# Matmuls without a reader in three waits, four buffers for layer 1's key chunks, and a square moved behind two copies, in a four-layer convolution sequence

## The chip, the cores and the metric

The kernel runs on one core of one Trainium2 chip, in float32 throughout. The metric is the device time of one execution in microseconds (us), given as the median of several runs. Nothing is shared with other cores.

## The reference

The input is `x`, four images (B = 4) of 192 channels on 64x64 pixels. Four layers follow each other, and each works on all four images:

```python
# layer 0: deformable 3x3 convolution gives q; k, v are 1x1; channel attention; then an MLP
xn  = layer_norm(xs);  q = deform_conv(xn, w_p, b_p, w_d)
out = softmax(qh @ l2norm(kh).T * temperature) @ l2norm(vh);  xs2 = xs + proj(out)
xs3 = xs2 + gelu(layer_norm(xs2) @ w_fc1 + b_fc1) @ w_fc2 + b_fc2
# layer 1: non-local block over all 4096 pixels, 96 channels
f1 = theta(x).T @ phi(x);  y = softmax(f1, -1) @ g(x);  x = W(y) + x
# layer 2: layer norm, qkv, attention in overlapping 8x8 windows (6 heads), gated MLP
y = conv1x1(ln_c(x), qkv);  win = unfold(y, 8, stride 6, pad 3)
out = fold(exp(q k^T + bias - max) v) / fold(sums);  x1 = x + hft(proj(out));  x = x1 + gated_mlp(ln_c(x1))
# layer 3: one masked depthwise 3x3 convolution whose weights depend on the image's mean
```

## The kernel before

The images are taken one after the other; `b` is the image. For each one the program makes layer 1's keys and values, runs layer 1, the windows of layer 2, and then the rest of layer 2 with layer 3. Beside that it works ahead on layer 0 of image b + 1: its gathers run inside layer 1 (`weave`), and its MLP (`mlp0`) inside the rest of layer 2 and layer 3 (`rest`). Image 0's own layer 0 has nothing beside it, and for the last image (b = 3) there is no next layer 0.

The order of instructions on each engine comes from a planner that works with costs and due times. Only the window loop is issued in the order in which it is written (`tc.manual_schedule()`). Tiles come from pools; a tile's buffer is free for the next tile of its tag when all readers and writers of the old one are done, and an instruction that writes it waits for that.

Four places matter here.

**The end of `mlp0`.** It goes over eight chunks of 512 pixels (`CN`). For each, `narrow(1)` (L821) and `narrow(0)` (L818) project the hidden layer back to 192 channels in PSUM tiles `o2` (shown as `o` in the profile), VectorE adds bias and residual (L825), and SyncE stores the chunk to the DRAM array `x_flat`, shown as `xd` (L844).

**`keys`** (L849). It reads the same array back in eight chunks `xk` of 384 KB (L855), from a pool `l1k` of two buffers, and makes the keys `ph` (two matmuls, L858, of 96 rows, 96 columns of the array and 512 moving columns) and the values `gx` (eight matmuls, L863, of 96 moving columns). For b = 1 and 2 it alternates with `offsets(b + 1)`, layer 0's first norm of the next image. For b = 0 and 3 it runs alone. For b = 0, 1 and 2 layer 1's gathers of layer 0 (L572, on POOL's queue) may begin at the same time, and the loads `xc` of layer 1's queries (L899) are on SyncE's queue.

**The end of `layer1`.** For each of 16 groups of queries the sums `y` (L976) are copied from PSUM by ScalarE (L982), then `finish` runs a reciprocal (L942), one matmul `pd`, a product, and two matmuls `wy` with an addition each (L950, L951).

**The start of `windows`** (L993). Window row 0 needs `norm(0)`, whose steps are the generator `layer_norm_steps`: mean by matmul `pm` (L360), difference on VectorE (L364), square on ScalarE (L367), variance by matmul `pv` (L339) and square root on ScalarE (L372), reciprocal on VectorE (L374), spreading by matmul `pb` (L348), product on VectorE (L382). `norm(wr, upto)` runs the generator up to the named step (MEAN, DIFFERENCE, SQUARE, VARIANCE, INVERSE). Then `project_rows` makes queries and keys (`qk`, L1064 and L1065, copied by ScalarE, L1068 and L1070). In the loop each row `wr` has three groups `g` of four windows and each group two pairs; `turned` makes the values `v` (L1139) and turned weights `t` (L1147), each in a PSUM buffer of tag "a" (two buffers, shared with `qk`), and ScalarE copies both out (`vs`, L1144, and `et`, L1149). At the start of row `wr` the norm of row `wr + 2` is run up to SQUARE.

Of the kernel before, what the change touches and what calls it, by code (L numbers as in the profile page):

```python
# [10 lines left out]
F32 = mybir.dt.float32  # L11
# [7 lines left out]
B, C, H, W = 4, 192, 64, 64  # L19
# [60 lines left out]
def conv_seq_kernel(ctx: ExitStack, tc: tile.TileContext, a, out: bass.AP):  # L80
# [437 lines left out]
    def gather(b, s, at, m2, kept=None):  # L518
# [166 lines left out]
            nc.scalar.copy(m2[rows, C + 2 * M + Q * q : C + 2 * M + Q * q + Q], pm[rows, M:C])  # L685
        yield

    def mlp0(b, m2, pool, sb, ps):


# [96 lines left out]
        for i in range(NCH):  # L787
            x = xs.pop(i)
            gl = pool.tile([128, 6, CN], F32, tag="gl", name=f"gl_{b}_{i}")

            def widen(ms):

                banks = [ps.tile([128, 2, HN], F32, tag="h", name=f"h_{b}_{i}_{ms[0]}_{q}") for q in range(2)]
                for j, m in enumerate(ms):
                    for q in range(2):
                        nc.tensor.matmul(
                            banks[q][:, j, :], lhsT=fc1[:, 0, bass.ts(m, 128)], rhs=hn[:, bass.ts(q, HN)], start=j == 0,
                            stop=False, skip_group_check=True,
                        )
                for j, m in enumerate(ms):  # L800
                    for q in range(2):
                        rows = slice(Q * q, Q * q + Q)
                        nc.tensor.matmul(
                            banks[q][:, j, :], lhsT=fc1[rows, 1, bass.ts(m, 128)], rhs=hn[rows, CN:], start=False, stop=True,
                            skip_group_check=True,
                        )
                for j, m in enumerate(ms):
                    for q in range(2):
                        nc.scalar.activation(
                            gl[:, m, bass.ts(q, HN)], banks[q][:, j, :], AF.Gelu, bias=fc1_bias[:, m : m + 1]  # L810
                        )

            def narrow(k):

                p = ps.tile([128, CN], F32, tag="h", name=f"o2_{b}_{i}_{k}")[:, 0 : HN if k else CN]
                for m in range(6):
                    if k == 0:
                        nc.tensor.matmul(p, lhsT=fc2[:, m, 0:M], rhs=gl[:, m, :], start=m == 0, stop=m == 5)  # L818
                        continue
                    for q in range(2):  # L820
                        nc.tensor.matmul(  # L821
                            p[Q * q : Q * q + Q], lhsT=fc2[:, m, M:C], rhs=gl[:, m, bass.ts(q, HN)], start=m == 0, stop=m == 5
                        )
                to = x[:, CN:] if k else x[:, 0:CN]
                nc.vector.scalar_tensor_tensor(to, p, VW["l0_bfc2"][:, k], to, ALU.add, ALU.add)  # L825


            if i + 1 < NCH:
                attend(i + 1)
            widen((0, 1))  # L830
            yield
            norm(i + 1, MEAN)
            widen((2, 3))
            norm(i + 1, SQUARE)
            yield
            widen((4, 5))
            norm(i + 1, VARIANCE)
            narrow(1)
            norm(i + 1, INVERSE)
            yield  # L840
            hn = norm(i + 1)
            narrow(0)
            for of, to in parts(x, HN, x_flat[b % 2], CN * i):
                nc.sync.dma_start(out=to, in_=of)  # L844
            if i + 2 < NCH:
                load(i + 2)
            yield
# [22 lines left out]
    def layer1(b, kv, beside):  # L870

        ph, gx = kv
        with ExitStack() as s:
# [83 lines left out]
            def next_scores(k):  # L957
                if k < NQ * NG:
                    i, g = divmod(k, NG)
                    if g == 0:  # L960
                        load(i)
                    score(i, g)
                    if g == NG - 1:
                        mbs[i] = negated_max(i)
# [3 lines left out]
            for k in range(NQ * NG):  # L968
                i, g = divmod(k, NG)
                if g == 0:  # L970
                    py = ps1.tile([P + 1, QN], F32, tag="y", name=f"y_{b}_{i}")
                ex = slot(i, g)
                nc.vector.tensor_tensor(ex, ex, mbs[i].unsqueeze(1).to_broadcast([128, G, QN]), ALU.add)  # L973
                nc.scalar.activation(ex, ex, AF.Exp)  # L974
                for t in range(G):
                    nc.tensor.matmul(  # L976
                        py, lhsT=gx[:, G * g + t, :], rhs=ex[:, t, :],
                        start=g == 0 and t == 0, stop=g == NG - 1 and t == G - 1,
                    )
                if g == NG - 1:  # L980
                    y = sb.tile([P + 1, QN], F32, tag="yn", name=f"yn_{b}_{i}")
                    nc.scalar.copy(y, py)  # L982
                    ends.append((k, i, y))
                next_scores(k + ahead)
                if ends and (k >= ends[0][0] + 2 or k == NQ * NG - 1):
                    finish(*ends.pop(0)[1:])
                if beside is not None:
                    beside(k + 1)
# [4 lines left out]
    def windows(b, oi, load_image):  # L993
# [3 lines left out]
        with ExitStack() as s:  # L997
# [225 lines left out]
            pos, ots, inv = {}, {}, {}  # L1223
            groups = -(-NWIN // WG)
            with tc.manual_schedule():
                norm(0)
                shared(0, 0)
                project_rows(0, 0)
                norm(1, SQUARE)
                project_rows(0, 1)  # L1230
                norm(1, VARIANCE)
                queries(0)
                inputs(0)
                norm(1)
                shared(1, 0)
                load(2)
                ex = exponentials(0, 0, scores(0, 0))
                due = None
                for wr in range(NWIN):
                    for g in range(groups):  # L1240
                        nxt = (wr, g + 1) if g + 1 < groups else (wr + 1, 0)
                        if wr + 2 < NWIN and g == 0:
                            norm(wr + 2, SQUARE)
                        if nxt[0] < NWIN:
                            sc = scores(*nxt)
                        if wr + 3 < NWIN and g == 1:
                            load(wr + 3)
                        if wr + 2 < NWIN and g == 2:
                            norm(wr + 2)
                        for pair in range(WG // 2):  # L1250
                            ops = turned(wr, g, pair, ex)
                            if due is not None:
                                outputs(*due)
                                if g == 0 and pair == 0:
                                    collect(wr - 1)
                            due = ops
                            if g == 0 and wr + 1 < NWIN:
                                project_rows(wr + 1, pair)
                            if wr > 0 and g == 1 and pair == 0:
                                inverses(wr - 1)  # L1260
                            if wr > 0 and g == 2:
                                finish(wr - 1, pair)
                        if wr + 2 < NWIN and g == 1:
                            norm(wr + 2, INVERSE)
                        if nxt[0] < NWIN:
                            ex = exponentials(*nxt, sc)
                        if g == 0 and wr + 1 < NWIN:
                            for i in (1, 2):
                                shared(wr + 1, i)
                            queries(wr + 1)  # L1270
                            inputs(wr + 1)
                        if g == 2 and wr + 2 < NWIN:
                            shared(wr + 2, 0)
                    if wr == 1:
                        load_image()
                outputs(*due)
                collect(NWIN - 1)
                inverses(NWIN - 1)
                for h in range(2):
                    finish(NWIN - 1, h)  # L1280
# [579 lines left out]
    for b in range(B):  # L1860
        with ExitStack() as s:
# [5 lines left out]
                m2 = stats.tile([M, C + 3 * M], F32, tag="m2", name=f"m2_{b + 1}")  # L1867
            with ExitStack() as s2:
                making = keys(
                    b, ph, gx, s2.enter_context(pool_of(name="l1k", bufs=2)),  # L1870
                    s2.enter_context(pool_of(name="l1kps", bufs=2, space=PSUM)),
                )
                if 0 < b < B - 1:
                    parts = offsets(b + 1, sb)
                    for _ in range(NCH):
                        next(parts)
                        next(making, None)
                    at = links(parts)
                for _ in making:
                    pass  # L1880
# [96 lines left out]
```

## Time and profile before

| what | value |
|---|---|
| time, median of 3 runs | 7006.99 us (6996.74 to 7022.0) |
| the profiled execution's own time | 6945.72 us |
| its span, first to last instruction | 6943.9 us |
| TensorE (PE) busy, weight loads (PEld) | 6255.0 us (90%), 4231.5 us |
| VectorE (DVE), ScalarE (ACT), GpSimd (POOL) | 4819.6, 3728.4, 2070.6 us |
| matmul records on PE | 45020 |
| mean granted TensorE clock | 0.928 |

One float32 matmul shows as two records in the profile: `keys` calls 64 matmuls at L858 over the four images, and the profile has 128 records of them. "PEclk" is the share of TensorE's full clock that was granted. A line of the timeline gives start, busy time, engine, source line, operation, tiles out<-in, form, and in brackets the idle time before it with what ended it. A line of the stretches gives the stretch, its length, busy time and count for each engine, the granted clock, the DMA engines' busy share and GB/s.

### The profile page before, as it was taken

The page shows a single profiled execution, that of the slowest core. Times are in us where ns is not written, and L with a number is a line of the kernel's source. Part 1 is how long each engine was busy: PE and PEld are TensorE (multiplying, and loading weights), DVE is VectorE, ACT ScalarE, POOL GpSimd, SP SyncE. Part 2 cuts the span into 40 slices and gives each one's busy share as a digit, 9 for nine tenths or more (in the row PEclk, how much of TensorE's full clock was granted, in tenths as well). Part 3 has the DMA queues.
Part 4 walks back from the last instruction along what each step waited for, and adds up shares of the span by engine and source line. Part 5 has one row for each costly group of instructions (what it writes and reads, how often), then busy time and mean ns, then how long its engine had stood idle before and what let it go on. Part 6 is the DMA issues. An engine that isn't in the chain of part 4 may idle for free.

```text
span 6943.9 us, 114885 instructions
## 1 busy us (share of the span) xinstructions
PE 6255.0 (90%) x45020; PEld 4231.5 (61%) x45020; DVE 4819.6 (69%) x7087; ACT 3728.4 (54%) x6214; POOL 2070.6 (30%) x2273
## 2 busy tenths in 40 slices
PE   7878999998987899999988889999998889999876
PEld 4545588885543468886644458887654457766532
DVE  3763199975677669984586849995577757755656
ACT  3763288864444368873544348884544325545331
POOL 2762077732200057751200017772210000012100
PEclk8889899998999899998989999999999979999998
DMA  7993267731010287761010067773010010010000
GB/s 234 302 350 115 74 196 231 232 118 35 24 29 14 72 258 222 231 196 35 10 42 14 28 215 221 226 230 96 13 30 21 19 48 12 12 36 12 4 7 20
DMA packets 362108, 743.43 MB, mean 107 GB/s; under 512 B 52647, under 2 KB 245335, under 8 KB 360798
## 3 DMA queue, kind: packets, MB, share of 16 engines
q0 software_dynamic: 95616, 469.38, 21.0%
q1 hardware_dynamic: 265950, 266.70, 12.9%
q8 instruction: 355, 5.82, 0.3%
q14 instruction: 187, 1.53, 0.1%
HBM read 628.06 MB, written 106.21 MB: 106 GB/s over the span
## 4 chain that ended last, share of the span: by engine, by line
PE 63%; DVE 19%; ACT 7%; DMA 6%; issue 4%; SPq 1%; POOL 0%; DVEq 0%; ACTq 0%; POOLq 0%
PE s L910 11%; PE y L976 10%; PE h L590 6%; DMA ring<-table,idx 3%; PE v L1139 2%; PE qk L1064 2%; DVE ha L1308 2%; PE qk L1065 2%; PE h L1508 2%; DVE ga L1308 2%; PE t L1147 1%; PE tp L858 1%; PE po L482 1%; DVE gate L1308 1%; DVE row L579 1%
## 5 line engine op out<-in xcount | busy, mean ns | idle before, releaser
L572 POOL DMA_INDIRECT ring<-table,idx x1188 | 1673.2, 1408 | 1019.5 <-DVE row L579 235.0
L910 PE MATMUL s<-ths,ph 96*128 96x256 f32 x4096 | 981.8, 385 | 9.0 <-ACT sc L912 4.3
L910 PEld LDWEIGHTS s<-ths,ph 96*128 96x128 f32 x4096 | 782.6, 193 | 148.6 <-ACT ths L904 16.9
L578 ACT ACTIVATE row<-ring,pos 128x384 f32<-128x384 f32 x1188 | 699.0, 610 | 252.6 <-DVE xo L583 159.3
L579 DVE SCALAR_TENSOR_TENSOR row<-ring,fr,row 128x384 f32<-128x384 f32 x1188 | 699.2, 613 | 115.9 <-ACT row L578 109.9
L976 PE MATMUL y<-sc,gx 128*97 128x256 f32 x3008 | 720.1, 379 | 0.0
L976 PEld LDWEIGHTS y<-sc,gx 128*97 128x97 f32 x3008 | 489.0, 164 | 125.7 <-issue 2.3
L582 ACT ACTIVATE xo<-row,pos 128x192 f32<-128x192 f32 x1188 | 503.8, 448 | 74.5 <-DVE row L579 42.4
L583 DVE SCALAR_TENSOR_TENSOR xo<-row,fr,xo 128x192 f32<-128x192 f32 x1188 | 463.9, 410 | 40.3 <-ACT xo L582 38.7
L590 PE MATMUL h<-ti,xo 128*128 128x192 f32 x2376 | 460.6, 329 | 5.8 <-DVE xo L583 5.8
L912 ACT COPY sc<-s 128x1024 f32<-128x1024 f32 x376 | 376.8, 1002 | 158.9 <-PE s L910 157.6
L973 DVE TENSOR_TENSOR sc<-sc,mbs 128x1024 f32<-128x1024 f32 x376 | 446.5, 1216 | 14.0 <-ACT mbs L936 13.7
L917 DVE TENSOR_TENSOR top<-top,sc 128x1024 f32<-128x1024 f32 x282 | 344.5, 1222 | 147.8 <-ACT sc L912 147.3
L590 PEld LDWEIGHTS h<-ti,xo 128*128 128x128 f32 x2376 | 404.7, 191 | 40.1 <-DVE xo L583 12.9
L974 ACT ACTIVATE sc<-sc 128x1024 f32<-128x1024 f32 x376 | 392.9, 1054 | 44.8 <-DVE sc L973 43.0
L1123 DVE TENSOR_REDUCE es<-ex 128x6 f32<-128x384 f32 x264 | 133.3, 546 | 404.2 <-ACT ex L1119 404.2
L1549 POOL COPY gate<-gate 128x192 f32<-128x192 f32 x12 | 4.2, 348 | 1106.1 <-ACT gate L1542 1106.1
L590 PE MATMUL h<-kept,xo 128*128 128x192 f32 x990 | 255.7, 391 | 80.2 <-DVE xo L583 73.4
L1308 DVE SCALAR_TENSOR_TENSOR ga<-gate,v,ga 128x1024 f32<-128x1024 f32 x234 | 299.7, 1281 | 7.2
L590 PEld LDWEIGHTS h<-kept,xo 128*128 128x128 f32 x990 | 180.4, 216 | 167.7 <-DVE xo L583 135.9
L976 PE MATMUL y<-se,gx 128*97 128x256 f32 x1088 | 260.4, 379 | 0.5 <-ACT yn L982 0.5
L1187 POOL TENSOR_TENSOR ot<-ot,ot 102x128 f32<-102x128 f32 x80 | 54.9, 699 | 624.0 <-ACT ot L1181 623.7
(384 smaller groups left out, 11615.0 us busy)
## 6 DMA issues: line engine op xcount, KB each, us to landing
ti<-table SPq DMA_DIRECT2D x396, 96.0 KB
table<-tt SPq DMA_DIRECT2D x24, 1056.0 KB
ring<-table,idx POOLq DMA_INDIRECT x1188, 5.1
xnd<-xn SPq DMA_DIRECT2D x4, 3270.0 KB
table<-kept SPq DMA_DIRECT2D x12, 1056.0 KB
table<-tt SPq DMA_DIRECT2D x44, 288.0 KB
xi<-in_x_dram SPq DMA_DIRECT2D x32, 384.0 KB
xk<-xd SPq DMA_DIRECT2D x32, 384.0 KB
```

The lines of the kernel that those rows point to most:

```text
L572: nc.gpsimd.indirect_dma_start(out=gt.rearrange("p r q c -> p (r q c)"), out_offset=None, in_=table[:, :], in_offset=bass.IndirectOffsetOn ...
L578: nc.scalar.activation(row, gt[:, :, 0, :], AF.Copy, scale=pos[:, t, 9 + tap : 10 + tap])
L579: nc.vector.scalar_tensor_tensor(row, gt[:, :, 1, :], fr[:, t, 9 + tap : 10 + tap], row, ALU.mult, ALU.add)
L582: nc.scalar.activation(xo[:, j, :], row[:, 0, :], AF.Copy, scale=pos[:, t, tap : tap + 1])
L583: nc.vector.scalar_tensor_tensor(xo[:, j, :], row[:, 1, :], fr[:, t, tap : tap + 1], xo[:, j, :], ALU.mult, ALU.add)
L590: nc.tensor.matmul(acc[m // 2][:, bass.ts(m % 2, C)], lhsT=xo.rearrange("p j c -> p (j c)")[:, bass.ts(m, 128)], rhs=tt, start=t == 0 and ...
L910: nc.tensor.matmul(p[:, t, :], lhsT=ph[:, bass.ts(G * g + t, 128)], rhs=ths[i], start=True, stop=True)
L912: nc.scalar.copy(to, p)
L973: nc.vector.tensor_tensor(ex, ex, mbs[i].unsqueeze(1).to_broadcast([128, G, QN]), ALU.add)
L974: nc.scalar.activation(ex, ex, AF.Exp)
L976: nc.tensor.matmul(py, lhsT=gx[:, G * g + t, :], rhs=ex[:, t, :], start=g == 0 and t == 0, stop=g == NG - 1 and t == G - 1,)
L1308: nc.vector.scalar_tensor_tensor(acc[:, b], src(tap, b), w[:, tap : tap + 1], acc[:, b], ALU.mult, ALU.add)
```

## The change

A helper `keep_warm(p, n)` issues `n` matmuls into a PSUM tile `p` that nothing reads: identity as weights, and as many columns of the constant `bias` as `p` is wide. It is called

- in `mlp0` after the last chunk's store: 12 matmuls of 384 columns into the tile of `narrow(0)`;
- in `layer1` after the last copy of `y`: 4 matmuls of 256 columns into that `y`;
- in `windows` during `norm(0)`: 2, 2 and 1 matmuls of 384 columns, into a tile of their own of tag "a", behind the mean, behind the variance, and behind the spreading.

Further, the pool `l1k` has four buffers in place of two for the first and the last image; and in window row 0 only the mean of `norm(2)` is run at the start, its difference and square follow behind `project_rows(1, 0)`.

```diff
+    def keep_warm(p, n):
+        m, width = p.shape
+        columns = bias.rearrange("p e h j -> p (e h j)")[:, 0:width]
+        for _ in range(n):
+            nc.tensor.matmul(p, lhsT=ident[:, 0:m], rhs=columns, start=True, stop=True)
...
                 nc.vector.scalar_tensor_tensor(to, p, VW["l0_bfc2"][:, k], to, ALU.add, ALU.add)
+                return p
...
-            narrow(0)
+            p = narrow(0)
             for of, to in parts(x, HN, x_flat[b % 2], CN * i):
                 nc.sync.dma_start(out=to, in_=of)
+            if i == NCH - 1:
+                keep_warm(p[:, 0:384], 12)
...
                     ends.append((k, i, y))
+                    if i == NQ - 1:
+                        keep_warm(py, 4)
...
             with tc.manual_schedule():
+                warm = ps2.tile([128, 512], F32, tag="a", name=f"warm_{b}")[:, 0:384]
+                norm(0, MEAN)
+                keep_warm(warm, 2)
+                norm(0, VARIANCE)
+                keep_warm(warm, 2)
                 norm(0)
+                keep_warm(warm, 1)
...
                         if wr + 2 < NWIN and g == 0:
-                            norm(wr + 2, SQUARE)
+                            norm(wr + 2, SQUARE if wr else MEAN)
...
                             if g == 0 and wr + 1 < NWIN:
                                 project_rows(wr + 1, pair)
+                            if wr == 0 and g == 0 and pair == 0:
+                                norm(2, SQUARE)
...
-                    b, ph, gx, s2.enter_context(pool_of(name="l1k", bufs=2)),
+                    b, ph, gx, s2.enter_context(pool_of(name="l1k", bufs=2 if 0 < b < B - 1 else 4)),
```

## The prediction

> **What bounds the kernel.** I read the page first: the slices of the span, then the chain that ended last.
>
> ```profile
> PEclk8889899998999899998989999999999979999998
> PE 63%; DVE 19%; ACT 7%; DMA 6%; issue 4%; SPq 1%; POOL 0%; DVEq 0%; ACTq 0%; POOLq 0%
> ```
>
> TensorE carries the chain, and its clock is below full in most slices. The mean of 0.928 stands for (1 - 0.928) x 2 x 6944 = 1000 us at half clock. So I asked the stretches where the half clock lies, for the keys of images 0 and 3 and for image 0's windows:
>
> ```profile
> 807.09:864.00 56.91, 56.21 (x164) 37.53 (x164) 4.46 (x8) 5.93 (x9) 9.46 (x10) 0.50 0.42 132
> 5621.22:5678.00 56.78, 56.22 (x165) 37.34 (x165) 4.46 (x8) 5.92 (x9) 0.00 (x0) 0.50 0.24 68
> 1556.86:1573.94 17.08, 11.86 (x42) 6.32 (x43) 3.84 (x8) 2.87 (x4) 5.01 (x8) 0.50 0.10 31
> 1573.94:1587.58 13.64, 9.80 (x157) 6.11 (x155) 7.77 (x11) 4.77 (x8) 4.25 (x14) 1.00 0.08 23
> 1587.58:1601.24 13.66, 12.87 (x60) 6.37 (x61) 2.38 (x3) 3.55 (x8) 1.78 (x5) 0.50 0.97 242
> 1601.24:1614.89 13.65, 11.05 (x294) 7.88 (x292) 8.98 (x13) 8.69 (x15) 3.54 (x12) 1.00 0.06 15
> 1614.89:1635.36 20.47, 20.14 (x146) 10.51 (x146) 5.09 (x7) 5.27 (x11) 2.23 (x7) 0.50 0.06 15
> 1635.36:1867.47 232.11, 216.06 (x4385) 145.47 (x4384) 142.79 (x204) 122.97 (x229) 57.89 (x162) 1.00 0.05 15
> ```
>
> PE is 99% busy through both key stages (56.2 of 56.9 and 56.8 us), all at 0.50: nothing but the clock bounds them. The windows lose it three times and then keep it for 232 us. The timelines show what a chunk costs cold (image 0) and warm (image 1):
>
> ```profile
> 801.69 0.75 DVE L825 SCALAR_TENSOR_TENSOR xa<-o,wide,xa 128x512 f32<-128x512 f32 x1 [4.83 <-PE o L818]
> 802.89 0.89 SPq L855 DMA_DIRECT2D xk<-xd  x2
> 807.09 3.73 PE L858 MATMUL tp<-xk,phiT 96*96 96x512 f32 x4 [5.44 <-DMA xk<-xd]
> 810.62 3.57 PE L863 MATMUL g<-gT,xk 96*128 96x96 f32 x16
> ...
> 2380.51 1.92 PE L863 MATMUL g<-gT,xk 96*128 96x96 f32 x16
> 2382.27 1.88 PE L858 MATMUL tp<-xk,phiT 96*96 96x512 f32 x4
> ```
>
> A cold chunk recurs every 6.78 us; a warm one takes half of the 3.42 us of `tp` and 54% of the 3.36 us of `g`, 3.5 us.
>
> [...] stretches at 0.50 and 1.00 only, their limits whole multiples of 3.41 us apart. [...] the drop at 1587.58 came after 1.7 us idle. I weighted every matmul's streaming time by rows x columns / 128 squared: the 100 windows that ended in a drop have at most 0.40 (median 0.21). Pure key chunks weigh about 0.56, enough to hold a full clock; they never raised it, while dense full windows elsewhere did. [...] the chunk issued at 814.22 moved nothing before 816 while the gathers moved 400 GB/s.
>
> **Part 1, `mlp0`.** 48 matmuls over four images. A 384-column matmul is two records; two warm `qk` records of 384 columns take 0.66 us (1684.26 to 1684.92), so 12 take 7.9 us. They wait for L825, which reads their tile. Queued behind them on PE is only the first key chunk, which waits for its DMA anyway:
> - b = 0: L825 ends 802.4, they end at 810.4; chunk landed 807.1: 3.3 us late.
> - b = 1: 2359.7, 2367.8; landed 2367.8: not late.
> - b = 2: 3996.8, 4004.9; landed 4004.9: not late.
> - b = 3: 5614.7, 5622.8; landed 5621.2: 1.5 us late.
>
> PE idles about 1.2 us ahead of them, too little for a drop, so the keys begin warm.
> - b = 0: eight chunks take 28.2 instead of 54.2 us: -26; two `th` -1; layer 1's first scores, cold until 870.8, -3.4; late start +3.3: -27.
> - b = 3: -26, `th` -0.9, scores cold until 5683.6 -2.8, +1.5: -28.
> - b = 1, 2: cold from 2367.8 to 2379.4 and 4004.9 to 4017.9, where `offsets` let it rise: half, -5.8 and -6.5.
>
> Sum -67. What follows is layer 1, bound by PE in steady state, so it shifts whole.
>
> **Part 2, buffers.** No DMA is added; the 32 loads move ahead on SyncE's queue. With two buffers a warm chunk (3.5 us) would wait for loads of about 4 us, and in image 0 for 816 and later. With four, three chunks follow the first at once, 1.6 MB by about 809 at the 250 GB/s seen there, ahead of the gathers. The `xc` loads behind them on SyncE's queue come later; the chunk that reuses the first buffer is issued near 814, lands near 823 and is needed near 825. Bounds: 0 if it is in time, +13 us if PE idles over 1 us in one window and the rest goes cold. I take +3.
>
> **Part 3, `layer1`.** Four 256-column matmuls at 0.45 us (34 `y` records took 7.58 us) are 1.8 us per image. They wait for the copy and lie beside the 1.75 us reciprocal; behind them only `pd`, which waits for that. Cost about 0, bounds 0 and +0.3.
>
> **Part 4, `norm(0)`.** Groups of 1.3, 1.3 and 0.66 us lie in PE's gaps of 1.7, 1.6 and 0.6 us (ahead of `pv`, `pb`, `qk`). With parts 3 and 4 the stretch from 1556.9 to 1573.9 runs warm: `pd`, one `wy`, `pm`, `pv`, `pb` and four `qk` halves save 0.5 + 0.5 + 1.1 + 0.3 + 0.7 + 2 = 5 us. In between lies 2.9 us with only `pd` and `wy`, which may still drop; then the dense matmuls raise the clock in one window. Bounds -5.3 and +1; I take -4.5, four times -18.
>
> **Part 5, the moved square.** The gap it removes:
>
> ```profile
> 1586.24 0.94 DVE L364 TENSOR_TENSOR d_l2n<-xr,pm_l2n 96x768 f32<-96x768 f32 x1
> 1587.27 0.84 ACT L367 ACTIVATE sq_l2n<-d_l2n 96x768 f32<-96x768 f32 x1 [2.00 <-DVE d_l2n L364]
> 1588.02 0.30 ACT L1144 COPY vs<-v 128x192 f32<-128x192 f32 x1
> 1588.37 1.59 PE L1064 MATMUL qk<-xs,qkvT 96*96 96x384 f32 x2 [2.49 <-ACT vs L1144]
> ```
>
> `qk` waits for a PSUM buffer, which waits for `vs`, queued on ScalarE behind the square, which waits for VectorE. Without that, `vs` ends at 1585.6 and `qk` starts at 1585.9, 2.5 us earlier. The square is next late: behind three VectorE steps of row 0's scores it ends near 1591.1, and the second pair's `vs` and `qk` wait, some 0.9 us. The scores at 1601.8 come at 1594.1 warm: -7.7. With a drop in one of five cases (some +8) I take -6, four times -24.
>
> **The third drop**, at 1614.89, has its own gap (1.70 us, PE waiting for VectorE's L382), which stays. In before it fell at the same place in all four images, but 4 windows after a rise, so the positions were not independent. Now they are; I give 45% that it is held. Warm, the stretch costs 11.2 (1675.1 to 1686.3) instead of 20.5 us: -9.3 x 0.45 x 4 = -17; bounds 0 and -37.
>
> **Sum.** -67 + 3 - 18 - 24 - 17 = -123 in the profiled execution. I take off 8 for waits of the added groups that no row shows: -115, to about 6830 (span 6829). The median of the runs shown lies 61 us above the profiled execution; I assume that this stays: 7007 - 115 = 6892.
>
> **Rivals.**
> - Partly held (chance 0.26): one of the pure key stages drops after a late chunk, which alone costs up to 20 us, and the windows find drops elsewhere. For it: the weight 0.56 allows only about 1 us idle in a window. Time about 6950.
> - The change doesn't do what it says (0.07): the planner places the added matmuls elsewhere, or the windows ahead are low enough for the drop to come all the same, with the extra matmuls mostly in idle time. Against it: L825 holds them at the right place. About 7000.
> - Slower (0.05): the drop comes ahead of the 12 matmuls, which then run at half clock, 15.8 us for waits of 4.5 to 8 us. [...] each image's keys start 8 to 11 us late and stay cold, +38; the five others add 3.3 more, the four 1.8: +5 per image, +20 in all: 7065. [...]
>
> **How the numbers follow.** The forecast case has 0.62. A measurement of this kernel tells about 0.3%, 21 us, from no change. The forecast's own bounds are 6845 to 6935; the partly held case stretches the range to 6968. Faster 0.88 (both upper cases), same 0.07, slower 0.05.
>
> **What would show it.** 168 more matmul records, 45188; mean clock about 0.96; half-clock time down from 1000 by some 230 us; eight key chunks in 28 to 30 us for b = 0 and 3; `qk`'s 2.5 us wait gone. It is wrong if the key stages show 0.50 again.

## The result and the profile after

The changed kernel took 6937 us (median of 4 runs, 6917 to 6953), the kernel before in the same comparison 7014 us. The ratio is 0.9897, with an interval of 0.9868 to 0.9926. That is 77 us less by the medians and, by the interval of the ratio, between 52 and 93 us (0.0074 and 0.0132 of 7014), where 115 were forecast.

The profiled execution of the changed kernel has a span of 6951.6 us. On its page, the granted clock and the chain that ended last:

```profile
PEclk8888989999999999999989999999998979999988
PE 65%; DVE 17%; ACT 7%; issue 4%; DMA 4%; SPq 1%; another core or an unknown queue 1%; POOL 1%; DVEq 0%; ACTq 0%; POOLq 0%
```

TensorE still carries the chain, and its mean clock went from 0.928 to 0.938, not to the 0.96 forecast. The clock's records, 200 before and 206 after, have 0.50 and 1.00 alone, so at half clock there are (1 - 0.938) x 2 x 6952 = 862 us. The stretches of the four key stages, from the first `tp` to the first `s` of layer 1 (columns: stretch, length, busy time and count of PE, PEld, DVE, ACT and POOL, clock, DMA share, GB/s):

```profile
859.92:909.10 49.18, 47.67 (x165) 30.90 (x163) 4.46 (x8) 5.94 (x9) 7.00 (x8) 0.62 0.42 134
2398.80:2514.00 115.20, 107.57 (x860) 56.19 (x860) 37.11 (x51) 39.84 (x78) 0.00 (x0) 0.95 0.66 211
4023.80:4133.30 109.50, 104.00 (x859) 54.95 (x859) 36.61 (x49) 39.84 (x78) 0.00 (x0) 0.99 0.69 220
5640.53:5694.50 53.97, 51.91 (x165) 34.83 (x163) 4.46 (x8) 5.93 (x9) 0.00 (x0) 0.56 0.26 68
```

Images 0 and 3, which were to take some 30 us each, took 49 and 54: the clock was lost again, at 868.2 and at 5646.8. The timelines show where, first TensorE in image 0:

```profile
852.08 8.01 PE L693 MATMUL o<-bias,ident 128*128 128x384 f32 x24 [0.84 <-DVE xa L832]
859.92 1.88 PE L868 MATMUL tp<-xk,phiT 96*96 96x512 f32 x4
...
863.40 1.88 PE L868 MATMUL tp<-xk,phiT 96*96 96x512 f32 x4
865.30 2.02 PE L873 MATMUL g<-gT,xk 96*128 96x96 f32 x16
868.26 3.73 PE L868 MATMUL tp<-xk,phiT 96*96 96x512 f32 x4 [0.93 <-ACT ph L869]
```

The twelve matmuls (L693) do what was said: they start 0.84 us after the MLP's last step and the first two chunks run warm (`tp` in 1.88 us). Then the second `tp`, begun at 863.40, is read late: ScalarE's `ph` runs only at 867.52, and the third chunk waits for it, since `tp` and `g` take turns in two PSUM buffers, so that each `tp` gets the one that the `tp` before it had. After 0.93 us of idle time the next `tp` takes 3.73 us, twice the 1.88: half clock. In image 3 it is SyncE's queue and then TensorE:

```profile
5634.78 0.73 SPq L865 DMA_DIRECT2D xk<-xd  x1
5638.53 1.26 SPq L1793 DMA_DIRECT2D out_dram<-out  x2
5639.89 4.62 SPq L865 DMA_DIRECT2D xk<-xd  x4
...
5645.69 2.57 PE L868 MATMUL tp<-xk,phiT 96*96 96x512 f32 x4 [1.52 <-DMA xk<-xd]
...
5648.05 2.29 PE L873 MATMUL g<-gT,xk 96*128 96x96 f32 x10
```

Between the load of the first chunk and that of the second stand two stores of `layer3`, which runs beside (`out_dram<-out`, L1793), issued only at 5638.53, when VectorE had finished their tile. So the second chunk is 1.52 us late, the clock falls within its `tp` (2.57 us is part warm, part cold), and no chunk after it raises it again.

The windows gained what was forecast. Image 0's own, with the change's groups in place:

```profile
1607.53 1.97 PE L693 MATMUL y<-bias,ident 128*97 128x256 f32 x8 [0.46 <-ACT yn L992]
1609.43 0.67 PE L954 MATMUL pd<-rd,ones 1*96 1x256 f32 x2
...
1614.54 2.04 PE L693 MATMUL warm<-bias,ident 128*128 128x384 f32 x4
```

and the stretches behind it (columns as above):

```profile
1607.00:1638.00 31.00, 27.05 (x243) 15.71 (x242) 15.21 (x21) 9.46 (x16) 10.90 (x23) 0.94 0.09 27
...
1661.00:1893.00 232.00, 218.60 (x4376) 146.16 (x4374) 141.82 (x203) 124.32 (x232) 58.87 (x159) 1.00 0.03 9
```

Before, this part lay at 0.50 three times; now it is at full clock but for one window of 3.4 us. From the end of layer 1's last `y` to the first `pp` the four images took 293.4, 309.3, 303.7 and 305.9 us, against 314.5, 333.7, 313.9 and 319.7 before.

The span nevertheless grew by 8 us against the profiled execution of before (6951.6 against 6943.9). Image 0's gathers, whose code is the same in both, ended (with the last `pg` matmul that uses them) at 642.1 us against 588.0. The first four runs below answer that.

### The profile page after: what moved, and what is told of

It is laid out like the page before. It is cut to its first block, busy times and chain, and to the rows that moved or that the text cites. A ratio compares the mean times of both kernels' runs of the same rounds, so it can differ in the third digit from the quotient of the medians.

```text
span 6951.6 us, 115213 instructions
## 1 busy us (share of the span) xinstructions
PE 6255.4 (90%) x45188; PEld 4235.5 (61%) x45188; DVE 4817.8 (69%) x7087; ACT 3725.4 (54%) x6214; POOL 2061.6 (30%) x2273
## 3 DMA queue, kind: packets, MB, share of 16 engines
q14 instruction: 187, 1.53, 0.1%
## 4 chain that ended last, share of the span: by engine, by line
PE 65%; DVE 17%; ACT 7%; issue 4%; DMA 4%; SPq 1%; another core or an unknown queue 1%; POOL 1%; DVEq 0%; ACTq 0%; POOLq 0%
PE s L920 11%; PE y L986 11%; PE h L590 7%; PE v L1151 2%; DVE ha L1328 2%; PE qk L1076 2%; PE h L1528 2%; DMA ring<-table,idx 2%; PE qk L1077 2%; DVE ga L1328 2%; PE po L482 2%; PE t L1159 1%; PE h L803 1%; DVE gate L1328 1%; PE zm L1539 1%
## 5 line engine op out<-in xcount | busy, mean ns | idle before, releaser
L579 DVE SCALAR_TENSOR_TENSOR row<-ring,fr,row 128x384 f32<-128x384 f32 x1188 | 696.9, 611 | 84.1 <-ACT row L578 56.8
L1533 ACT ACTIVATE z<-h,bias_fc1T 128x512 f32<-128x512 f32 x192 | 118.0, 687 | 230.2 <-PE h L1530 229.9
```

The costliest lines, as they stand in the source:

```text
L579: nc.vector.scalar_tensor_tensor(row, gt[:, :, 1, :], fr[:, t, 9 + tap : 10 + tap], row, ALU.mult, ALU.add)
```

## The experiments

Each ratio is against the kernel before on the same chip, with its 95% interval. Three groups of four ran on three chips, in the order of the next sections (keys and third drop cross: `psum4_pool` and `best` on the second, `no_mlp0`, `psum4`, `two_buffers` and `third_only` on the third); the kernel before took 7008 us on the first, 6917 and 6919 on the others.

### The two kernels again, and the two halves of the change

`again_before` and `again_after` are the two kernels unchanged. `keys_part` keeps what concerns the keys:

```diff
-                    if i == NQ - 1:
-                        keep_warm(py, 4)
...
-                warm = ps2.tile([128, 512], F32, tag="a", name=f"warm_{b}")[:, 0:384]
-                norm(0, MEAN)
-                keep_warm(warm, 2)
-                norm(0, VARIANCE)
-                keep_warm(warm, 2)
                 norm(0)
-                keep_warm(warm, 1)
...
-                            norm(wr + 2, SQUARE if wr else MEAN)
+                            norm(wr + 2, SQUARE)
...
-                            if wr == 0 and g == 0 and pair == 0:
-                                norm(2, SQUARE)
```

`windows_part` keeps exactly those lines and goes back in the others:

```diff
-            if i == NCH - 1:
-                keep_warm(p[:, 0:384], 12)
...
-                    b, ph, gx, s2.enter_context(pool_of(name="l1k", bufs=2 if 0 < b < B - 1 else 4)),
+                    b, ph, gx, s2.enter_context(pool_of(name="l1k", bufs=2)),
```

> The kernel before, unchanged, for a second profile. The profiled execution of the changed kernel spent 54 us more in image 0's gathers, whose instructions stand in the same order in both kernels, and about 10 us more in layer 1 of images 0, 1 and 2 in steps at which PE, ACT and DVE stand idle with no releaser that the profile shows. Theory A (these stalls come and go from execution to execution, whatever the kernel): this profile may show them too, its span then lies near 7000 us, and the ratio of times is 1.00. Rival B (the added instructions bring the stalls): this profile has none, its span is near 6944 us with layer 1 of image 0 at 691 us from first score to last y.

Measured: ratio 1.0008 (0.9995 to 1.0022), span 6982.5 us. The gathers ended at 639.0 us in this execution, and layer 1 of images 0, 1 and 2 (first `s` to last `y`) took 703.1, 707.1 and 702.1 us, against 690.7, 694.9 and 694.2 in the first one. The unchanged kernel thus has the same longer gathers. In the waits of the stretch from 120 to 600 us, rows with "remote", waits whose end the profile puts down to nothing of this core, stand out, of which the first profile has none (engine, line, waited for: us in total, times, longest):

```profile
ACT xo L582 <- remote: 44.9, 10, 7.6
```

The changed kernel's profile has the same row:

```profile
ACT xo L582 <- remote: 66.1, 14, 12.6
```

So 50 us of gathers and some 30 us in layer 1 are not the change's: the first profile of before was an execution without these waits, and that of after one with them.

> The changed kernel again, for a second profile and a tighter ratio: 0.989 of before, between 0.986 and 0.992. Theory A: the stalls in image 0's gathers differ from the first profile of this kernel (54 us), perhaps to none, with a span of 6890 to 6960 us. Rival B: they are there again at the same places, 54 us and about 10 us in layer 1 of each of images 0 to 2. In both: the key chunks of images 0 and 3 go back to half clock after one to three chunks.

Measured: ratio 0.9877 (0.9844 to 0.991), span 6929.9 us, 52.6 less than `again_before`. Image 3's keys held the clock this time (30.5 us), image 0's did not (51.7 us).

> Only the 12 matmuls behind layer 0's MLP and the four key buffers; no matmuls in layer 1 and in the norm, no moved square. Theory (the gain is time at half clock that is avoided, and the key stages of images 0 and 3 lose the clock again after few chunks): a gain of 10 to 25 us, ratio 0.9965 to 0.9985. Rival (the recorded forecast, keys worth 64 us): ratio 0.991. Rival (the keys part costs, since the added matmuls hold the first chunks back by 3.3 and 1.5 us and the clock is lost anyway): ratio 1.000 or above.

Measured: ratio 0.9972 (0.9955 to 0.999), 20 us of 7008. Images 0 and 3 took 51.1 and 53.9 us for their keys, both at half clock for the greater part.

> Only the matmuls in layer 1's end and in layer 2's first norm, and the moved square; two key buffers, no matmuls behind the MLP. Theory (half clock avoided in the windows, which the first pair of profiles puts at 21, 25, 10 and 14 us for the four images): a gain of 55 to 75 us, ratio 0.989 to 0.992. Rival (the recorded forecast): 59 us, 0.9916. Rival (most of it comes from the keys): under 30 us, ratio above 0.996.

Measured: ratio 0.992 (0.9901 to 0.9939), 56 us. The four stretches of windows sum to 1206.3 us, against 1254.7 in `again_before`.

What follows: 0.28% and 0.80% sum to 1.08%, within the intervals of the whole, whose two measurements are 1.03% and 1.23%. The windows brought about what was forecast for them, the keys under a third.

### What in the windows: the square or the matmuls

`square_only` has of the whole change only the moved square, `norm_only` only the added matmuls behind `y` and in `norm(0)`:

```diff
 square_only
+                            norm(wr + 2, SQUARE if wr else MEAN)
...
+                            if wr == 0 and g == 0 and pair == 0:
+                                norm(2, SQUARE)
...
 norm_only
+                    if i == NQ - 1:
+                        keep_warm(py, 4)
...
+                norm(0, MEAN)
+                keep_warm(warm, 2)
+                norm(0, VARIANCE)
+                keep_warm(warm, 2)
                 norm(0)
+                keep_warm(warm, 1)
```

> The moved square alone: no matmul is added anywhere, the chunks of keys keep two buffers, and layer 1 has no added matmuls. Theory S (the square matters through the wait it removes): qk's 2.5 us wait behind the copy vs goes in all four images, the second pair waits some 0.9 us in its place, and the second drop of the clock goes where the square was what emptied PE's window; the stretch from the end of layer 1's last y to the first pp comes down by 5 to 9 us per image, 20 to 36 us in all, ratio 0.995 to 0.997. Rival N (without the added matmuls the first norm still leaves the clock down, so that the wait is removed in a stretch that is cold anyway and the drop comes elsewhere): 0 to 10 us, ratio 0.9985 to 1.000.

Measured: ratio 0.9958 (0.994 to 0.9975), 29 us of 6917. The longest wait of `qk` for `vs` is 1.1 us, where it was 2.5.

> The added matmuls behind layer 1's last y and in the first norm alone: the square stays where it was, no matmuls are added behind layer 0's MLP, and the chunks of keys keep two buffers. Theory S (the two parts add up): the 57 us that both save together are split, so with 20 to 36 us for the square there remain 20 to 35 us here, ratio 0.995 to 0.997, and qk's wait of 2.5 us is still seen. Rival T (the two parts need each other: a clock that is held through the norm is lost again at the 2.5 us wait): no more than 12 us, ratio 0.998 to 1.000, with a drop at that wait in each image.

Measured: ratio 0.9953 (0.993 to 0.9976), 33 us; `qk` still waits 2.5 us for `vs`.

What follows: theory S in both. The two sum to 62 us, and `windows_part` has 56 with an interval of 43 to 69: as far as these intervals tell they add up, and neither needs the other.

### What loses the clock in the keys

`psum4_pool` is the changed kernel with four PSUM buffers in place of two for `tp` and `g`, and another queue for image 3, `no_mlp0` is `psum4_pool` without the twelve matmuls, `psum4` has the buffers alone, `two_buffers` is the changed kernel with two buffers for the chunks:

```diff
 psum4_pool (psum4: the second edit alone)
-            nc.sync.dma_start(out=x, in_=x_drams[b % 2][:, :, cols])
+            (nc.gpsimd if b == B - 1 else nc.sync).dma_start(out=x, in_=x_drams[b % 2][:, :, cols])
...
-                    s2.enter_context(pool_of(name="l1kps", bufs=2, space=PSUM)),
+                    s2.enter_context(pool_of(name="l1kps", bufs=2 if 0 < b < B - 1 else 4, space=PSUM)),
...
 no_mlp0 (on top of both)
-            if i == NCH - 1:
-                keep_warm(p[:, 0:384], 12)
...
 two_buffers
-                    b, ph, gx, s2.enter_context(pool_of(name="l1k", bufs=2 if 0 < b < B - 1 else 4)),
+                    b, ph, gx, s2.enter_context(pool_of(name="l1k", bufs=2)),
```

> The changed kernel with two more edits for the keys: four PSUM buffers in place of two for tp in images 0 and 3, so that a late ScalarE or VectorE does not stop PE, and in image 3 the loads of the chunks from POOL's queue, so that they do not stand behind the stores of layer 0's outputs on SyncE's. Theory K (the keys lose the clock because one wait of 0.9 to 1.7 us ahead of a chunk takes the window below what it needs): the idle times of 0.93 us in image 0 and 1.52 us in image 3 go, both key stages stay at full clock, 28 to 33 us each instead of 47 to 54, and the kernel is 15 to 45 us below the changed one: ratio 0.980 to 0.986. Rival L (pure key chunks are too light to keep the clock whatever the waits): both stages drop all the same within 10 us of the start, ratio 0.987 to 0.990 as for the changed kernel.

Measured: ratio 0.986 (0.9829 to 0.9892), 97 us of 6917, span 6796.3 us at a mean clock of 0.951. Both key stages stay at full clock, 29.4 us each, and TensorE's timeline has no idle time within them. By place this is told from the changed kernel; by the ratio (0.9897 and 0.9877 there) it is not. The stores on SyncE's queue are those of `layer3`, not of layer 0 as the expectation has it.

> The kernel with four PSUM buffers and image 3's loads from POOL's queue, but without the twelve matmuls behind layer 0's MLP. Theory K (the twelve matmuls hold the clock over the 5 us wait for the first chunk; the buffers then keep it through the chunks, and pure chunks can't raise it again): without the matmuls the clock is lost in that wait, and the keys of images 0 and 3 stay at 0.50 for all of their 50 us, so the kernel is 40 to 55 us slower than with them, ratio 0.992 to 0.995. Rival B (chunks that follow each other without a wait are dense enough to raise the clock themselves, so the buffers alone suffice): the clock rises within two windows and the loss is 10 to 20 us, ratio 0.987 to 0.990.

Measured: ratio 0.9953 (0.9935 to 0.997), span 6862.4 us. Its key stages of images 0 and 3, in the columns above, are those of before:

```profile
803.50:860.30 56.80, 56.23 (x165) 37.37 (x165) 4.46 (x8) 5.93 (x9) 9.45 (x10) 0.50 0.41 132
5559.40:5616.20 56.80, 56.21 (x164) 37.35 (x164) 4.92 (x10) 5.92 (x9) 3.82 (x6) 0.50 0.24 75
```

The keys of all four images sum to 344.3 us here and to 281.3 in `psum4_pool`: the twelve matmuls are worth 63 us where nothing after them loses the clock, and without them the buffers bring nothing for the keys. The ratios say the same, 0.93% or 64 us apart, and their intervals don't overlap. Theory K; pure chunks did not raise the clock.

> The changed kernel with four PSUM buffers for tp in images 0 and 3, and image 3's loads on SyncE's queue as they were. Theory K by place: image 0 holds its clock (its wait was for ScalarE), 26 to 29 us for the eight chunks; image 3 still has the wait of some 1.5 us for its second chunk behind the stores of layer 0 and drops if that wait falls badly in the windows, so 30 to 50 us there; ratio 0.984 to 0.988. If POOL's queue alone were what mattered: image 0 drops as in the changed kernel, ratio near 0.989.

Measured: ratio 0.9889 (0.9855 to 0.9924), span 6812.5 us. Both stages held, image 3 in spite of its second chunk being late, where the expectation had 30 to 50 us:

```profile
812.50:842.40 29.90, 29.04 (x166) 20.08 (x164) 4.46 (x8) 5.93 (x9) 6.93 (x8) 1.00 0.68 219
5534.00:5564.80 30.80, 29.04 (x166) 20.05 (x164) 4.46 (x8) 5.93 (x9) 0.00 (x0) 1.00 0.41 111
```

TensorE's timeline of image 3 shows the wait that it survived:

```profile
5538.79 1.96 PE L868 MATMUL tp<-xk,phiT 96*96 96x512 f32 x4 [1.20 <-DMA xk<-xd]
5540.59 1.92 PE L873 MATMUL g<-gT,xk 96*128 96x96 f32 x16
```

> The changed kernel with two buffers for the chunks of keys in place of four. The prediction's part 2: with two, a warm chunk waits for its load, the clock is lost in the second or third chunk, and the keys of images 0 and 3 take 45 to 54 us each: 5 to 20 us slower than with four, ratio 0.990 to 0.992. If the four buffers do nothing, because the changed kernel loses the clock at other waits anyway: ratio 0.988 to 0.990, the same.

Measured: ratio 0.9907 (0.9881 to 0.9933). By the ratio it can't be told from the changed kernel; by place it can. Image 0's third chunk waits for its load, and the stage is cold from there, 55.6 us:

```profile
819.61 2.85 PE L868 MATMUL tp<-xk,phiT 96*96 96x512 f32 x3 [5.53 <-DMA xk<-xd]
```

Image 3 held its clock with two buffers (31.8 us, where 45 to 54 were expected): its longest wait was 0.91 us.

### The third drop

`third_only` is the changed kernel with two matmuls in the wait ahead of row 1's scores; `best` is `psum4_pool` with the same two lines:

```diff
+                        if wr == 1 and g == 0:
+                            keep_warm(ps2.tile([128, 512], F32, tag="a", name=f"warm1_{b}")[:, 0:384], 2)
```

> The changed kernel with two more 384-column matmuls in the wait ahead of layer 2's second row, and nothing done for the keys. If the third drop is owed to that wait: the drop goes in three or four images and the stretch from layer 1's last y to the first pp comes down by 3 to 8 us each from 295 to 305 us, ratio 0.984 to 0.987. If it is owed to more than that wait: it comes back one window later, ratio 0.987 to 0.990 as for the changed kernel.

Measured: ratio 0.9882 (0.9848 to 0.9915), as the changed kernel. The third drop is gone in all four images, and yet the four stretches of windows sum to 1203.2 us, no less than in the other kernels with parts 3 to 5 (the table below). Image 0's keys held (30.6 us), image 3's did not (53.8 us):

```profile
5535.17 2.51 PE L868 MATMUL tp<-xk,phiT 96*96 96x512 f32 x4 [1.39 <-DMA xk<-xd]
5537.47 3.57 PE L873 MATMUL g<-gT,xk 96*128 96x96 f32 x16
```

> As the kernel with four PSUM buffers and image 3's loads from POOL's queue, and two more 384-column matmuls in the wait ahead of layer 2's second row (before the norm of row 3), for the third drop. If that drop is owed to the wait there alone: it goes in three or four images, 10 to 30 us less than without, ratio 0.976 to 0.982. If the window is low for more than that wait: the drop stays or comes one window later, and the two are equal within 0.2%.

Measured: ratio 0.9825 (0.9796 to 0.9853), 121 us of 6917, 6793 us as median. It is the fastest kernel of the study, and beats the kernel before and, by intervals that don't overlap, `square_only` and `norm_only`; against the changed kernel itself there is only the comparison across chips (0.9877 to 0.9897). From `psum4_pool` (0.986) it isn't told apart.

### All runs by stage

Lengths in us of the profiled executions. Keys: first `tp` to first `s`. Windows: end of layer 1's last `y` to first `pp`, four images, and the half clock in them by the clock's records. Each line is one execution; the runs of one kernel differ (`psum4`: 6805 to 6869 us over six, `best`: 6787 to 6806 over five), so a stage that held in a profile need not hold in every run.

| kernel | keys, image 0 | keys, image 3 | windows, sum | half clock there |
|---|---|---|---|---|
| before | 57.0 | 56.8 | 1281.9 | 266 |
| again_before | 45.5 | 56.8 | 1254.7 | 207 |
| keys_part | 51.1 | 53.9 | 1254.8 | 217 |
| square_only | 38.6 | 56.8 | 1226.2 | 158 |
| norm_only | 45.7 | 56.8 | 1236.4 | 151 |
| windows_part | 38.7 | 56.8 | 1206.3 | 91 |
| after | 49.2 | 54.0 | 1212.3 | 112 |
| again_after | 51.7 | 30.5 | 1203.0 | 85 |
| two_buffers | 55.6 | 31.8 | 1206.2 | 86 |
| third_only | 30.6 | 53.8 | 1203.2 | 90 |
| psum4 | 29.9 | 30.8 | 1208.3 | 98 |
| psum4_pool | 29.4 | 29.4 | 1193.2 | 65 |
| best | 30.1 | 29.4 | 1203.1 | 91 |
| no_mlp0 | 56.8 | 56.8 | 1198.8 | 86 |

## Why the prediction was right, and where it was not

The direction, the place and the mechanism were right: what was gained is half clock that became full clock. Each timed run has its clock and span on record, and (1 - clock) x 2 x span gives its time at half clock. Its mean fell from 1023 us before to 808 in `again_after`, 887 in `windows_part` and 966 in `keys_part`. Half of each fall, 107, 68 and 28 us, covers the 82, 56 and 16 us that the mean span fell by; what is left over, 11 to 25 us, may be what the additions cost themselves; that is not shown. The size was wrong: a third of the 115 us did not come, and that was one term.

- **Part 1, the keys (-67).** This is the term that was mis-sized. Its arithmetic holds: `no_mlp0` against `psum4_pool` gives 63 us, the twelve matmuls took 8.01 us for the 7.9 estimated, they began 0.84 us behind the MLP in image 0 and 1.15 in the others (1.2 estimated, "too little for a drop": the first `tp` behind them took 1.88 to 1.96 us in all four images, full clock), and the first chunk came later behind the MLP's last matmul by 3.0 and 1.3 us in images 0 and 3 (`again_after` against `again_before`; 3.3 and 1.5 estimated). What failed is the step "so the keys begin warm", taken as warm to the end. In the changed kernel and `keys_part`, five of six key stages of images 0 and 3 (three profiles) lost the clock in the second or third chunk, and `keys_part` brought 20 us, not 67.
- **Part 2, the buffers (+3).** The upper bound named the case, a wait of over 1 us in one window, "and the rest goes cold", but it was the usual one and at +13 too cheap: against the 29.4 us of `psum4_pool` it cost 20 to 25 us per stage. The working looked at the loads behind one another only. It missed that in image 3 SyncE's queue has two stores of `layer3` between the first chunk's load and the second's, and that `tp` and `g` go through two PSUM buffers, which ScalarE and VectorE must free in time. In image 0 the reasoning was right: with two buffers the third chunk waited 5.53 us.
- **How long a wait may be.** All clock changes of a trace lie on one grid of 3.413 us (to within 0.005 us for the 200 of `before` and the 206 of the changed kernel), so it can be told how much of a wait lies in one window. Of the longest waits within the key stages that had the twelve matmuls, these were survived: 0.82 us in one window (`two_buffers`, image 3), 0.87 (`again_after`, image 3), 0.92 (`psum4`, image 3) and 0.95 (`third_only`, image 0). These lost the clock: 0.86 (after, image 0), 1.25 (`again_after`, image 0), 1.39 (`third_only`, image 3), 1.47 and 1.53 (`keys_part`, images 3 and 0), 1.52 (after, image 3), and the 5.53 us of `two_buffers` in image 0, longer than a window. `psum4`'s wait of 1.20 us fell on two windows, with 0.92 and 0.27 us; that it was survived fits this order of lengths, but no run moved the position on purpose. So the edge lies near 0.9 us in one window, and 1.25 or more was lost each time, near the prediction's "about 1 us idle in a window". That figure was an estimate from the trace of before: a key chunk's weight of 0.56 falls to 0.40, the most that a window ending in a drop had there, when 1 - 0.40/0.56 of 3.41, or 1.0 us, is idle. Image 0's waits for ScalarE and VectorE (0.93, 1.25 and 1.53 us) are waits for PSUM buffers; in the changed kernel's first profile the single one of 0.93 us was enough, and the clock stayed down for 37.5 us.
- **Part 3 (about 0).** Right: the four matmuls end at 1609.5, and `pd` starts at 1609.43 by the timeline, 0.17 us behind the reciprocal's end, where it was 0.06 in `again_before`.
- **Parts 4 and 5 and the third drop (-18, -24, -17: 59 in all).** `windows_part` gave 56 (43 to 69). The square alone gave 29 (17 to 42) for the 24, the wait that takes its place is 1.1 us for the 0.9:

```profile
1638.78 0.84 ACT L367 ACTIVATE sq_l2n<-d_l2n 96x768 f32<-96x768 f32 x1 [1.32 <-DVE d_l2n L364]
1639.53 0.30 ACT L1156 COPY vs<-v 128x192 f32<-128x192 f32 x1
...
1639.88 0.89 PE L1076 MATMUL qk<-xs,qkvT 96*96 96x384 f32 x2 [1.12 <-ACT vs L1156]
```

  The added matmuls gave 33 (17 to 48) for the 18 of part 4. A held third drop is not in that: in `norm_only`'s profile it stands in all four images. The stretch with only `pd` and `wy`, which the forecast said may still drop, did so in 19 of the 28 stages of windows of the seven profiles with parts 3 to 5 and without the two matmuls of `third_only`, in 18 of them for one window of 3.4 us.

  The chance of 45% that the third drop is held was near: 13 of these 28 stages have no drop between 45 and 53 us after `y`. Its worth of -9.3 shows only where like is set beside like. Some stages have a drop of 10 us some 22 us after `y`. That one lies ahead of the two matmuls of `third_only` and `best`, so it is not their doing; it stands in 5 of the 8 stages of these two kernels and in 7 of the 28. Among the stages without it, the 10 with the third drop take 303.7 us on average, the 11 without it 296.5, and the three of `third_only` and `best` 297.2. So a third drop that is held is worth some 7 us, few stages as these are. In the sums over all stages this can't be seen (1203 us with the two matmuls against 1204 on average without, half clock 90 and 91 us against 89).
- **The 61 us.** That the median lies as far above the profiled execution after the change was wrong (6937 against a span of 6951.6). The profile of before was an execution without the waits on "remote". Since the forecast took only the difference from the profile and the level from the median, it did no harm to the number, but the spans of the two first profiles can't be compared.
- **The signs.** The 45188 records and the shorter wait of `qk` came as said. The time at half clock fell from 1000 to 862 us, not by 230. The mean clock of 0.96 did not follow from the forecast's own figures: with 770 us left at half clock in 6829 us it would be 0.944. The sign for wrong, key stages at 0.50 again, came too, and it was right about the part that failed: what happened is the rival "partly held" for the keys, in more stages than the one it counted on, with the windows as in the forecast. Its 6950 us was nearer than the forecast's 6892.

**What stays open.** In image 0 the late `ph` and `gx` of the changed kernel were seen only in executions that have waits without a visible cause. The four PSUM buffers ran on chips without such waits, where `third_only` held image 0's clock with two. So what the PSUM buffers are worth in image 0 is argued, not shown. In image 3 the second chunk's wait comes from SyncE's queue: it is 0.51 to 1.52 us in the six profiles that load from there behind the twelve matmuls, and none in `psum4_pool` and `best`, which load from POOL's queue. That this wait costs the clock rests on the order of lengths above, for the one pair of kernels that differs in this queue alone, `psum4` and `psum4_pool`, held the clock in both. Nor was a chunk load ahead of the stores on SyncE's queue tried; POOL's queue took its place.

## What to carry to other kernels

In this kernel, raising the clock ahead of a stage paid in full only where no later wait in that stage took much more than 0.9 us of one window. So follow each buffer that the stage recycles and each queue that its loads share, with other stages' stores too, before counting the whole stage as warm. Where a drop is removed, compare stages that ran alike up to the edit: the 7 us of the third drop were hidden in the sums by drops that lie ahead of the edit and differ from execution to execution. Take two profiles of the same kernel before explaining a difference in span.

## What the runs showed of the hardware

- **Waits that went with one chip.** On the first chip the gathers of image 0 ended 639 to 645 us after the start in all four kernels and layer 1 of images 0 to 2 took 702 to 709 us; on the two others 586 to 595 and 687 to 696 us, with no row "remote" in the gathers' waits. By the means this makes 52 + 3 x 13 = 91 us, the 90 us between the medians of the kernel before (7008 against 6917 and 6919). The first profile of before, for which no chip is on record, has no such row either, and its own time of 6945.72 us lies below all four timed runs of its comparison (6997 to 7028). So whether the waits belong to the chip or come and go is not settled, and their cause isn't known.
- **Pure chunks can raise the clock, in one position.** The prediction said that they never did. In image 0 of `again_before`, `windows_part`, `square_only` and `norm_only` they did, 20 to 34 us after the drop, each time during the `tp` that follows a `th` (the matmul for layer 1's queries). `square_only`, TensorE's timeline:

```profile
823.12 1.06 PE L910 MATMUL th<-xc,thetaT 96*96 96x256 f32 x2
823.98 3.58 PE L866 MATMUL tp<-xk,phiT 96*96 96x512 f32 x4
827.39 1.92 PE L871 MATMUL g<-gT,xk 96*128 96x96 f32 x16
```

  A chunk recurs every 6.78 us, nearly two windows of 3.41 us, so each `tp` lies almost the same in the windows until a `th` of 0.86 us shifts it; here the window that ended at 827.4 held `tp` alone. Image 0 of the changed kernel shows the same without a `th`. Two windows are 6.83 us, so each chunk begins 0.05 us earlier in them: its `tp` started 0.25 us behind a window's start at 875.26, 0.09 at 895.58 and 0.03 at 902.35, and at the end of that last window, which `tp` filled but for this, the clock rose (`after`, TensorE's timeline):

```profile
902.35 3.57 PE L868 MATMUL tp<-xk,phiT 96*96 96x512 f32 x4
905.75 1.92 PE L873 MATMUL g<-gT,xk 96*128 96x96 f32 x16
```

  In image 3, where every `th` comes behind the last chunk, all six profiles without the twelve matmuls stayed cold to the end (56.8 us), and so did image 0 of `no_mlp0`, where the four buffers have put the `th` there too. A `th` in between is not enough: the first profile of before has two, and stays cold. In it neither of the two put a `tp` over a whole window. This fits the reading; no run moved the phase on purpose.
